# Second phase by groups of four batches: q and k of four batches per product, h1 parts in a ring, mean of x1 from a sum, plain projections at the end

## The chip, the cores and the metric

The kernel runs on one core of one Trainium2 chip. The metric is the device time of one execution in microseconds (us), as the median of several runs. Lower is better.

## The reference, cut to what matters

The input `x` has 128 batches of 128 rows and 512 columns. Two layers follow each other. The first normalises each row, mixes the rows of a batch with the 128x128 matrix `adj`, and multiplies by a 512x512 weight. The second is masked attention with 8 heads of 64 columns, a projection, and another normalisation. All is in float32.

```
h = relu(layernorm(x))
x1 = x + (adj @ h) @ w0 + b0                      # per batch
h1 = relu(layernorm(x1))
q, k, v = split(h1 @ w_qkv)                       # 8 heads of 64
s = softmax(where(adj == 0, -inf, q @ k.T / 8))   # per head, 128x128
o = concat(s @ v) @ w_proj + b_proj
out = x1 + o + layernorm(o) * gamma + beta
```

## The kernel before

**Order.** The kernel doesn't issue its instructions in the order of the source. Every piece of work is declared with `op(...)` or `dma(...)`: its engine, an estimated duration, what it reads and writes, and either a place in TensorE's time (`at`) or a due time (`due`). `Plan.schedule` then plays the pieces against those estimates and picks, on each engine, the ready piece with the earliest due time; `Plan.emit` issues them in that order. On the chip the order of each engine is fixed. Only semaphores for data and for reused buffers make an engine wait; `after=` and the estimates only shape the order.

**Buffers.** `G` lists pools of tile names. A `buf("qk", ...)` takes a name of its pool when the planner comes to it and gives it back after its last use. `t0` to `t29` are 2 KB per partition, `f0` to `f9` 4 KB, `b0` to `b7` are the eight banks of PSUM.

**Precision.** A large product is made from three products of shortened float32 values (`float32r`, called `HALF` here). The left side is split into parts h, l and s (`split_left`: one ScalarE copy, two VectorE instructions), the weights likewise (`split_weights`). `times_weights` (L398) runs 3 x 4 matmuls of 512 columns into two PSUM tiles, and `sum_up` (L414) joins these with two VectorE instructions.

**Phase 1** (`phase1`) takes the batches one after the other: load, statistics, relu, mix (L439), product with `w0` (L405), sum (L416, L418), and a store of x1 to a scratch tensor in device memory (`x1d`). In the first four batches the product is made in plain float32 instead: four matmuls per batch, which the profile shows as eight records (L448).

**Phase 2** (`phase2_pair`, L474) takes two batches at a time. x1 is loaded again (`xn in`). Statistics come from two passes of ScalarE over each batch: a sum (L374) and a sum of squares about the mean (L376), each followed by a read of the accumulator. h1 is transposed by a trip through device memory (`exchange`, L459: one DMA out, four in) and a 32x32 block transpose on VectorE (L503), and is split into hh, hl and hs of a pair (L505, L509, L506). Then come:

- q and k (L522): 4 products, each 2 halves x 3 parts x 4 = 24 matmuls of 256 columns (two batches side by side), 96 per pair; sums L529 and L530;
- v (L405 with `wv`): 12 matmuls of 512 columns per batch; sums L536, L537;
- scores (L550, small tiles), the mask added (L559), the maximum (L564), the exponentials (L571: eight per batch), the division (L576);
- the trip of the softmax through device memory (`e out`, `e in`) and a transpose (L585); in the last pair four TensorE transposes per half instead (L593);
- attend (L603, small tiles), two pairs later, then the split L392, L393, L394, the projection (L405 with `wA`), the sums L416, L418, and the tail of the batch: `x1 in`, statistics (L360 to L370), L619 to L625, store. In the last two pairs gamma and the last addition are on VectorE (L627, L629).

`T1` and `T2` are the planner's periods for a batch of phase 1 (3.7) and a pair of phase 2 (26.6). All DMAs are issued from SP.

Of the kernel before, what the change touches and what calls it, by code (L numbers as in the profile page):

```python
# [52 lines left out]
class Op:  # L53
    __slots__ = ("eng", "us", "fn", "at", "due", "prio", "bufs", "preds", "succ", "n", "ready", "start", "end", "id", "lands", "what", "tiled")


class Plan:

# [8 lines left out]
    def op(self, eng, us, fn, r=(), w=(), at=None, due=None, lands=None, what="", after=(), tiled=False):  # L67
        o = Op()
        o.eng, o.us, o.fn, o.at, o.due, o.lands, o.what, o.tiled = eng, us, fn, at, due, lands, what, tiled
        o.id, o.preds, o.succ, o.bufs = len(self.ops), set(after), [], []  # L70
# [29 lines left out]
    def schedule(self):  # L100
        p = self.p
        for o in self.ops:
            o.n, o.ready = len(o.preds), 0.0
            for x in o.preds:
                x.succ.append(o)
# [10 lines left out]
        free = dict.fromkeys(self.ENGINES, 0.0)  # L116
        for o in self.ops:
            if not o.n:
                heapq.heappush(pending[o.eng], (0.0, o.id))
        events, t, pipe, order, tiled = [0.0], 0.0, 0.0, [], False  # L120
# [68 lines left out]
    "rate": 200e3, "landing": 2.2, "lag": 0.15, "slack": 0.4, "slot": 0.15, "turn": 0.15, "stay": 2.0,  # L189
# [5 lines left out]
def kernel(  # L195
# [35 lines left out]
    def named(prefix, *numbers):  # L231
# [4 lines left out]
        "x": group(named("t", 0, 8) + named("t", 24, 27) + ["t29"]), "h0": group(named("t", 27, 29)), "y": group(named("t", 10, 16)),  # L236
        "raw": group(named("t", 16, 20)), "raw0": group(named("t", 20, 24)),
        "qk": group(named("t", 0, 8)), "xn": group(named("t", 8, 10)), "op": group(named("t", 10, 16)),
        "hx": group(named("t", 16, 18)), "ht": group(named("t", 18, 20)),
        "v": group(named("t", 20, 25) + ["t29"]), "o": group(named("t", 25, 27)), "x1b": group(named("t", 27, 29)),  # L240
        "hp": group(named("f", 0, 5)), "s": group(named("f", 5, 7)), "sx": group(named("f", 7, 8)),
        "pT": group(named("f", 8, 10)),
        "st": group(named("m", 0, 8)), "st2": group(named("l", 0, 4)), "mx": group(named("n", 0, 8)),
# [103 lines left out]
    broadcast(b0_b, b0, -4)  # L347


    def stats(srcs, how, place, due=None, plain=False):  # L350

        w = len(srcs)
        t = buf(place, [P, 24])
# [335 lines left out]
```

## Time and profile before

| | |
|---|---|
| median of 3 runs | 2218.36 us (2216.33 to 2219.66) |
| the profiled execution | 2219.66 us, span of its instructions 2217.9 us |
| granted TensorE clock in it | 0.997 |
| busy | PE 99%, PEld 88%, DVE 84%, ACT 68%, POOL 63% |
| DMA | 53.3% of 16 engines, 170 GB/s |

The times inside the profile belong to one execution. PE is TensorE's matmuls, PEld its weight loads, DVE VectorE, ACT ScalarE, POOL GpSimd, SP the engine that issues the DMAs. Matmuls overlap in their pipeline and the ends of their records are modelled. So the time of a stretch is read from the starts: the start of the next row less the start of this one. A row `x96` of the timeline is a merged run of 96 instructions.

### The profile page before, as it was taken

Reading aid. Unit: us, or ns where it says so; the run is one execution under the profiler, and the core shown is the slowest. Engines: PE = TensorE matmul, PEld = TensorE weight load, DVE = VectorE, ACT = ScalarE, POOL = GpSimd, SP = SyncE. Lnnn points to the kernel's source line nnn. Section 1 sums busy time; section 2 is a strip of 40 time slices with the busy share of each in tenths; the row PEclk is TensorE's granted clock in tenths of the full one; section 3 lists DMA queues with packets and bytes.
Section 4 is the critical chain, followed back from the end, with each engine's and each line's share of the span. In section 5 each row is a group of like instructions: output and inputs, shape, how many; then the busy total and the mean of one; then the engine's idle time right before and its main releaser. Section 6 shows DMA issues by size and latency. Waiting matters only on the chain.

```text
span 2217.9 us, 46318 instructions
## 1 busy us (share of the span) xinstructions
PE 2195.8 (99%) x15907; PEld 1946.6 (88%) x15907; DVE 1858.7 (84%) x3127; ACT 1518.1 (68%) x4368; POOL 1401.6 (63%) x1154
## 2 busy tenths in 40 slices
PE   9999999999999999999999999999999999999997
PEld 7888888888888999888899999999888899998995
DVE  6877777776888888888888888888888988888888
ACT  7887777766666666666666666666666666666662
POOL 4444444433677766767776666677777777666666
PEclk9999999999999999999999999999999999999999
DMA  5544444534555656555555555555555555555553
GB/s 193 172 153 148 144 144 143 172 133 134 172 171 172 189 175 192 180 178 181 177 175 182 185 181 174 180 177 174 179 174 183 182 176 172 180 172 174 184 166 95
DMA packets 278875, 376.43 MB, mean 170 GB/s; under 512 B 30960, under 2 KB 161136, under 8 KB 278640
## 3 DMA queue, kind: packets, MB, share of 16 engines
q1 hardware_dynamic: 278640, 373.48, 53.3%
q8 instruction: 125, 2.05, 0.4%
q14 instruction: 110, 0.90, 0.1%
HBM read 206.64 MB, written 166.72 MB: 168 GB/s over the span
## 4 chain that ended last, share of the span: by engine, by line
PE 97%; DVE 1%; DMA 1%; POOL 1%; issue 0%; SPq 0%; POOLq 0%; ACT 0%; DVEq 0%; ACTq 0%
PE b L405 47%; PE b L522 34%; PE b L550 6%; PE b L603 5%; PE b L439 5%; DMA t<-in_x_dram 1%; PE b L448 1%; POOL t L621 0%; DVE f L559 0%; DMA t<-x1d 0%; POOL t L625 0%; SPq L261 0%; DVE l L370 0%; DVE l L360 0%; POOL t L619 0%
## 5 line engine op out<-in xcount | busy, mean ns | idle before, releaser
L522 PEld LDWEIGHTS b<-f,wqk 128*128 128x128 f32 x6144 | 753.8, 192 | 18.6 <-ACT t L392 9.8
L522 PE MATMUL b<-f,wqk 128*128 128x256 f32 x6144 | 768.3, 284 | 0.0
L405 PE MATMUL b<-wA,t 128*128 128x512 f32 x3024 | 761.3, 398 | 6.6 <-DVE t L394 2.8
L405 PEld LDWEIGHTS b<-wA,t 128*128 128x128 f32 x3024 | 547.4, 188 | 121.1 <-DVE t L393 4.0
L571 ACT ACTIVATE f<-f,n 128x128 f32<-128x128 f32 x1024 | 396.8, 391 | 2.2
L405 PE MATMUL b<-wv,f 128*128 128x512 f32 x1536 | 363.9, 392 | 2.6 <-DVE f L506 1.6
L405 PEld LDWEIGHTS b<-wv,f 128*128 128x128 f32 x1536 | 287.9, 188 | 67.2 <-ACT f L505 1.9
L576 POOL TENSOR_TENSOR f<-f,n 128x1024 f32<-128x1024 f32 x128 | 245.5, 1918 | 144.0 <-DVE n L575 138.0
L392 ACT ACTIVATE t<-b 128x512 fp32r<-128x512 f32 x252 | 149.6, 594 | 207.4 <-PE b L603 104.4
L433 POOL TENSOR_TENSOR t<-t,b_b 128x512 f32<-128x512 f32 x128 | 166.7, 1303 | 181.2 <-ACT t L431 181.0
L529 ACT ACTIVATE t<-b 128x512 f32<-128x512 f32 x256 | 152.2, 594 | 183.9 <-PE b L522 183.8
L621 POOL TENSOR_TENSOR t<-t,t 128x512 f32<-128x512 f32 x128 | 174.4, 1362 | 160.4 <-DVE t L418 156.6
L619 POOL TENSOR_TENSOR t<-t,beta_b 128x512 f32<-128x512 f32 x128 | 167.9, 1312 | 137.1 <-DMA t<-x1d 137.1
L393 DVE TENSOR_TENSOR t<-b,t 128x512 fp32r<-128x512 f32 x252 | 171.6, 681 | 77.1 <-ACT t L392 77.1
L530 DVE TENSOR_TENSOR t<-b,t 128x512 f32<-128x512 f32 x256 | 172.8, 679 | 75.3 <-PE b L522 72.2
L418 DVE TENSOR_TENSOR t<-b,t 128x512 f32<-128x512 f32 x252 | 173.9, 690 | 49.4 <-PE b L405 48.8
L571 ACT ACTIVATION_READ_ACCUMULATOR f<-f,n 128x1 f32 x1024 | 194.6, 190 | 0.0
L509 POOL TENSOR_TENSOR f<-t,f 128x512 fp32r<-128x512 f32 x128 | 178.7, 1415 | 20.8 <-ACT f L505 16.6
L376 ACT ACTIVATE junk<-t,m 128x512 bf16<-128x512 f32 x250 | 180.1, 720 | 6.2
L624 POOL TENSOR_TENSOR t<-t,gamma_b 128x512 f32<-128x512 f32 x124 | 161.1, 1299 | 32.7 <-ACT t L623 32.6
L394 DVE SCALAR_TENSOR_TENSOR t<-t,b 128x512 fp32r<-128x512 f32 x252 | 170.7, 677 | 0.0
L625 POOL TENSOR_TENSOR t<-t,t 128x512 f32<-128x512 f32 x124 | 160.4, 1293 | 9.6
(84 smaller groups left out, 3029.5 us busy)
## 6 DMA issues: line engine op xcount, KB each, us to landing
t<-x1d SPq DMA_DIRECT2D x256, 256.0 KB, 4.1
d<-f SPq DMA_DIRECT2D x126, 512.0 KB, 3.2
f<-d SPq DMA_DIRECT2D x504, 128.0 KB, 3.1
t<-in_x_dram SPq DMA_DIRECT2D x128, 256.0 KB, 2.8
x1d<-t SPq DMA_DIRECT2D x128, 256.0 KB, 2.0
d<-t SPq DMA_DIRECT2D x128, 256.0 KB, 3.2
t<-d SPq DMA_DIRECT2D x512, 64.0 KB, 3.3
out_dram<-t SPq DMA_DIRECT2D x128, 256.0 KB, 2.2
```

The costliest lines, as they stand in the source:

```text
L376: op("ACT", 0.91, lambda n=n, src=src: nc.scalar.activation(junk.ap, src.ap, AF.Square, bias=t.ap[:, n:n + 1], accum_out=t.ap[:, 4 + n:5 + ...
L393: op("DVE", 0.69, lambda: nc.vector.tensor_tensor(l.ap, p.ap, h.ap.bitcast(F32), op=ALU.subtract), r=[p, h], w=[l], what=name + "l")
L394: op("DVE", 0.69, lambda: nc.vector.scalar_tensor_tensor(s.ap, h.ap.bitcast(F32), UP, p.ap, op0=ALU.mult, op1=ALU.subtract), r=[p, h], w=[ ...
L405: nc.tensor.matmul(p.ap, lhsT=t[0].ap[:, c] if t[1] is None else t[0].ap[:, c, t[1], :], rhs=w.ap[:, m, c, :], start=start and c == 0, sto ...
L418: op("DVE", 0.69, lambda: nc.vector.tensor_tensor(dst.ap, b.ap, dst.ap, op=ALU.add), r=[b], w=[dst], due=at + 4.5, what=what)
L509: op("POOL", 1.35, lambda n=n, ht=ht: nc.gpsimd.tensor_tensor(hl.ap[:, :, n, :], ht.ap, hh.ap[:, :, n, :].bitcast(F32), op=ALU.subtract), ...
L522: nc.tensor.matmul(p.ap[:, half, :], lhsT=wqk.ap[:, which, c, col:col + P], rhs=src.ap[:, c].rearrange("p b n -> p (b n)"), start=start an ...
L530: op("DVE", 0.69, lambda r=r, b=b: nc.vector.tensor_tensor(r.ap, b.ap, r.ap, op=ALU.add), r=[b], w=[r], due=tg + 5, what="qkB")
L571: nc.scalar.activation(v[:, h], v[:, h], AF.Exp, bias=mx.ap[:, h:h + 1], scale=scale, accum_out=mx.ap[:, H + h:H + h + 1])
L576: op("POOL", 1.93, lambda heads=heads, mx=mx: nc.gpsimd.tensor_tensor(heads().rearrange("p h q r -> p q h r"), heads().rearrange("p h q r ...
L619: op("POOL", 1.32, lambda x1=x1: nc.gpsimd.tensor_tensor(x1.ap, x1.ap, beta_b.ap, op=ALU.add), r=[beta_b], w=[x1], due=tl, what="beta")
L621: op("POOL", 1.32, lambda x1=x1, o=O[n]: nc.gpsimd.tensor_tensor(x1.ap, x1.ap, o.ap, op=ALU.add), r=[O[n]], w=[x1], due=tl + (3 if left > ...
```

## The change

Phase 2 takes four batches at a time (`phase2_group`), `T4` = 52.3 to the planner.

- q and k: 8 products per group, each 3 parts x 4 = 12 matmuls of 512 columns over four batches, 96 per group. The moving operand is cut from one tile `hp`, a ring of three pairs. It takes two of the pairs, so it reads four runs of 128 columns.
- h1's parts live in this ring. The transpose after the exchange is in place, and hs is made from hh and hl.
- The mean of x1: phase 1's last addition also writes the sum of its row (`accum_out`); one small VectorE instruction per group scales four sums; ScalarE's sum pass of phase 2 is gone.
- The softmax (`scores_of`) and what follows it (`rest_of`) are declared apart, one group after each other. In the plan `e in` waits for a product of q and k, or for the scores. `e in` lands in the tile that is then transposed in place. `s` and `pT` share four tiles.
- The last three pairs project in plain float32 and with one sum. Gamma and the last addition are on VectorE in them, and in the last pair x1 + o too.
- Pools are cut anew, mostly smaller (`mx` 8 to 4, `st` 8 to 3, `op` 6 to 4). The planner's DMA rate goes from 200e3 to 300e3. In all the built program has 3072 q and k matmuls for 6144, 4488 for 4560 of L405's kind, and 24 plain ones.

```diff
-    "rate": 200e3, "landing": 2.2, ...
+    "rate": 300e3, "landing": 2.2, ...
...
-        "qk": group(named("t", 0, 8)), "xn": group(named("t", 8, 10)), "op": group(named("t", 10, 16)),
-        "hx": group(named("t", 16, 18)), "ht": group(named("t", 18, 20)),
...
-        "hp": group(named("f", 0, 5)), "s": group(named("f", 5, 7)), "sx": group(named("f", 7, 8)),
-        "pT": group(named("f", 8, 10)),
+        "qk": group(named("t", 0, 8)), "v": group(named("t", 8, 14)), "op": group(named("t", 14, 18)),
+        "o": group(named("t", 18, 20)), "xn": group(named("t", 20, 22)), "hx": group(named("t", 22, 24)), "x1b": group(named("t", 24, 26)),
+        "s": group(named("f", 0, 4), fifo=False), "pT": group(named("f", 0, 4), fifo=False), "raw1": group(named("f", 2, 4)),
...
+    hp = const.tile([P, 3, 2, 3, C, P], HALF, name="hp")
-    T1, T2 = 3.7, 26.6
+    T1, T4 = 3.7, 52.3
...
+            op("DVE", 0.75, lambda: nc.vector.scalar_tensor_tensor(dst.ap, b.ap, 1.0, dst.ap, op0=ALU.mult, op1=ALU.add, accum_out=mean(i)),
+               r=[b], w=[dst, (means, i)], due=at + 4.5, what=what)
...
+    HP = {(i, m): Buf(group([f"hp{i % 6}{m}"]), lambda _, i=i, m=m: hp[:, i // 2 % 3, i % 2, m]) for i in range(B) for m in range(3)}
...
+            exchange(flat[n], C * R, 256, "h1")(flat[n])
+            op("DVE", 0.71, lambda h1=h1: nc.vector.transpose(h1.ap, h1.ap), w=[h1], what="h1T")
...
+            op("DVE", 0.7, lambda h=h, l=l, s=s: nc.vector.scalar_tensor_tensor(s(), h().bitcast(F32), 1.0 / K, l().bitcast(F32), op0=ALU.mult, op1=ALU.subtract),
...
-        for g, (kind, m) in enumerate((k, m) for m in range(2) for k in range(2)):
-            r = QK[kind, m] = buf("qk", [P, 2, 2 * P])
-            def run(p, src, which, start, stop, kind=kind, m=m):
-                for half in range(2):
-                    col = kind * D + (2 * m + half) * P
-                    for c in range(C):
-                        nc.tensor.matmul(p.ap[:, half, :], lhsT=wqk.ap[:, which, c, col:col + P],
-                                         rhs=src.ap[:, c].rearrange("p b n -> p (b n)"),
...
+        for g in range(8):
+            kind, m = g % 2, g // 2
+            r = QK[kind, m] = buf("qk", [P, D])
+            def run(p, which, start, stop, col=kind * D + m * P):
+                for c in range(C):
+                    nc.tensor.matmul(p.ap, lhsT=wqk.ap[:, which, c, col:col + P], rhs=hp[:, pick, :, which, c, :],
+                                     start=start and c == 0, stop=stop and c == C - 1)
...
+            if g == 4:
+                gate = [b.writers[-1][1]]
...
+            if rank > 2:
+                parts = split_left(PO[n], "op")
+                a, b = times_weights([(q, None, lambda q=q: q.ap) for q in parts], wA1, at_proj[n], "proj")
+                sum_up(o, a, b, bp_b, at_proj[n], "o")
+            else:
+                y, a = buf("op", [P, C, P]), buf("ps", [P, D])
+                op("ACT", 0.6, lambda y=y, p=PO[n]: nc.scalar.copy(y.ap, p.ap), r=[PO[n]], w=[y], what="oph")
+                def plain(a=a, y=y):
+                    for c in range(C):
+                        nc.tensor.matmul(a.ap, lhsT=y.ap[:, c], rhs=raw2[c].ap, start=c == 0, stop=c == C - 1)
+                op("PE", 3.43, plain, r=[y] + raw2, w=[a], at=at_proj[n], what="proj")
+                op("DVE", 0.69, lambda o=o, a=a: nc.vector.tensor_tensor(o.ap, a.ap, bp_b.ap, op=ALU.add), r=[a, bp_b], w=[o], due=at_proj[n] + 4, what="o")
```

## The prediction

> **What bounds the kernel now.** I read busy times first, then the windows by stage, then TensorE's timeline, which gives the durations.
>
> ```profile
> PE 2195.8 (99%) x15907; PEld 1946.6 (88%) x15907; DVE 1858.7 (84%) x3127; ACT 1518.1 (68%) x4368; POOL 1401.6 (63%) x1154
> ```
>
> TensorE is busy all the time. A modelled matmul end makes that number weak alone, so the windows (start, end, length, then busy time of each engine) must show where it holds:
>
> ```profile
> 488.00:553.00 65.00, 63.18 (x503) 57.66 (x503) 45.16 (x70) 45.93 (x139) 17.49 (x13) 1.00 0.46 143
> 554.00:2177.00 1623.00, 1622.19 (x12673) 1462.68 (x12671) 1412.06 (x2310) 1092.80 (x3384) 1136.73 (x915) 1.00 0.57 177
> 2177.00:2217.90 40.90, 25.52 (x156) 17.88 (x152) 36.27 (x62) 12.13 (x43) 27.94 (x23) 0.92 0.27 87
> ```
>
> In the 1623 us of the steady second phase TensorE misses 0.8 us; VectorE is next with 87%. The first phase is the same (465.4 of 466.0). Only the entry of phase 2 (1.8 us) and the last 41 us have TensorE waiting; there VectorE is busy 36.3 of 40.9. One period of a pair, from scores to scores:
>
> ```profile
> 1001.75 2.06 PE L550 MATMUL b<-t,t 64*128 64x128 f32 x32
> 1003.74 1.97 PE L603 MATMUL b<-f,t 128*64 128x128 f32 x32
> 1005.63 2.18 PE L522 MATMUL b<-f,wqk 128*128 128x256 f32 x16
> 1007.65 1.09 PE L405 MATMUL b<-wA,t 128*128 128x512 f32 x4
> 1008.58 3.99 PE L522 MATMUL b<-f,wqk 128*128 128x256 f32 x32
> 1012.41 2.02 PE L405 MATMUL b<-wA,t 128*128 128x512 f32 x8
> 1014.27 5.92 PE L522 MATMUL b<-f,wqk 128*128 128x256 f32 x48
> 1020.02 2.94 PE L405 MATMUL b<-wA,t 128*128 128x512 f32 x12
> 1022.79 5.65 PE L405 MATMUL b<-wv,f 128*128 128x512 f32 x24
> 1028.37 2.06 PE L550 MATMUL b<-t,t 64*128 64x128 f32 x32
> ```
>
> By starts, a pair takes 26.62 us: scores 1.99, attend 1.89, q and k 2.02 + 3.83 + 5.75 = 11.60, projections and v (48 matmuls) 11.13. So 512 columns cost 0.232 us and 256 columns 0.120 us (3.83 / 32). The first 16 after attend take 2.02 for 1.92: a change from small to full tiles costs about 0.1.
>
> The plain product of phase 1 and the end, with idle time and its releaser in brackets:
>
> ```profile
> 27.90 3.65 PE L448 MATMUL b<-t,t 128*128 128x512 f32 x8
> 31.38 1.05 PE L439 MATMUL b<-adjT,t 128*128 128x128 f32 x8
> ...
> 2177.10 1.19 PE L405 MATMUL b<-wA,t 128*128 128x512 f32 x4
> 2179.50 5.44 PE L405 MATMUL b<-wA,t 128*128 128x512 f32 x20 [1.21 <-DVE t L393]
> 2208.79 1.20 PE L405 MATMUL b<-wA,t 128*128 128x512 f32 x4 [2.13 <-DVE t L394]
> ```
>
> A plain product is 3.48 us by starts. The end: from 2177.10 to TensorE's last end, 2209.99, are 32.9 us. The work in them is 72 matmuls of 512 columns (16.7), two attends (3.8) and 16 transposes (2.4), 22.9 together. So 10.0 us are waits, for the split of the left side on VectorE above all; 7.9 us follow TensorE's last end.
>
> **What the Trainium skill says.** (1) "TensorE: Matmul & The Clock Gate", section "Back-to-back issue gap", gives the isolated gap as N / 2.4 + 2.5 ns: 109 ns for 256 columns, 216 for 512. Two of 256 for one of 512 would then save the fixed 2.5 ns alone. The trace differs: 120 and 232, so 8 ns are saved. The trace's numbers are used. (2) "SBUF — State Buffer", section "Who interferes with whom": a VectorE instruction with two SBUF inputs and a GpSimd instruction that reads SBUF lock each other out for a whole instruction. The trace agrees: L506 has two SBUF inputs and takes 679 ns in the median, but up to 2344:
>
> ```profile
> L506 DVE SCALAR_TENSOR_TENSOR f<-f,t x128: 645/679/2344, 486.4 to 2144.7; 128x512 fp32r<-128x512 f32 x128
> ```
>
> The same table gives TensorE its own ports for the moving operand and the weights. (3) "VectorE: DVE Perf Modes", section "Two Vector instructions with no wait between them": an op that writes out its accumulator is two instructions. No VectorE row before does this; ScalarE's read of an accumulator takes 189 ns.
>
> **The change part by part.**
>
> *q and k.* Before, 96 x 0.120 = 11.52 per pair, 23.04 per four batches. After, 96 x 0.232 = 22.27. That saves 0.77 per group, 24.7 over 32 groups. In the built program's order, attend of the second pair stands apart from its scores (scores, 4 of v, 8 of q and k, 4 of v, attend), so a group has three returns from small tiles for two: +0.1, 3 us in 31 groups. Net **-22**. The new period should be 192 x 0.232 + 7.76 + 0.24 = 52.5 us for 53.24. The moving operand now comes in four runs of 128 columns; no row before reads so. I take nothing for it (own port, one column after the other); from 0 to 4 ns per matmul, as one run's start can hardly cost more than the 8 ns won, it is 0 to +12.
>
> *Mean from a sum.* ScalarE loses 128 x (0.623 + 0.189) = 104 us, TensorE nothing, as ScalarE has 530 us to spare in 1623. VectorE gains a read in each of 128 batches of phase 1: priced as ScalarE's 0.19, 24 us, so 75% there becomes 80%, beneath a TensorE that is 99.9% busy; at 0.06 or 0.3 it is still hidden. Per group one small VectorE instruction (0.15). Cost 0; without the cover it is 0.19 per batch.
>
> *Ring, in-place transposes, hs from hh and hl.* The same instructions of about the same length: VectorE 1412 us / 61 pairs = 23.1 per pair, 46.5 per group of 52.5, 88%. ScalarE falls to 63%, GpSimd stays at 71%. hs now waits for hl (GpSimd, 1.4) also. The second pair of a group can't be split until v of the pair in its place is done: that is 12 v, 24 others and scores before its first use, over 10 us for some 5 us of splitting. Cost 0, up to 0.4 per group.
>
> *e in moved.* SP issues 52 DMAs per group, at 0.43 us 22 of 52.5. The first pair's e in stands behind the second pair's first e out, which waits for a GpSimd division; behind it wait a store and the next h1 out. From that division to both transposed tiles: 8 issues (3.4), landing (3.1), two transposes (2.5), 9 us. By the built order attend follows q and k's start by 31.6 us (128 matmuls and an attend), the division by about 15. Slack some 7 us: cost 0. If the queue is held by that much, each us late is a us per group. The 1 MB for the second copy of w_proj lands in a stretch with DMA 57% busy: 0.
>
> *Entry of phase 2.* Nothing to attend yet, so group 1's q and k follow after 37.4 us (96 + 48 matmuls, scores). Before, 1.8 us of waits for h1's parts; after 0 to 6, I take 2: 0.
>
> *The end.* Six batches plain: 6 x (3.48 - 12 x 0.232) = +4.2. VectorE loses l, s and one sum in each, 6 x 2.05 = 12.3, and gains gamma, out (two batches) and x1 + o: 4.4. The waits of 10.0 become about 3 (0 to 8), since a plain product needs only a ScalarE copy. After TensorE's last end: one sum less, about -1 of 7.9. Together **-4** (-8 to +2).
>
> Sum: -22 + 0 - 4 = **-26**. The span becomes 2192; the profiled execution (2219.66, 1.76 beyond its span) lies 1.3 above the median of the runs shown, so the median goes from 2218.4 to **2192**.
>
> **The rivals.**
>
> *A, forecast:* TensorE stays the bound; 2192, own range 2181 to 2200.
>
> *B, part of it lost:* small waits come back in each group, since the pools are smaller and the stretch of v, projection and scores (about 21 us) bunches VectorE's work. At 0.4 us per group, 13 us: 2205. For it: VectorE at 88%. Against: at 87%, TensorE missed 0.8 us in 1623.
>
> *C, slower:* VectorE falls out of step around the scores. Two scores take four PSUM banks and attend two of eight; v and projections take two per product. Banks come free only by VectorE's mask and sum instructions, in their order. One port collision there (L506 shows up to 1.7 us) holds every matmul behind the next bank. It decides at 0.8 us per group, where the gain is gone; at 1.3 per group, 42 us less the 26, it is 2234. For it: an order from estimates that know no lock, now with hs behind hl. Against: the order before came from the same estimates and held.
>
> *D, the wide product isn't cheaper:* the four runs cost the 8 ns. Then only the end gains, +3 for the third return: 2217. Against: nothing in the profile shows such a cost.
>
> **How the numbers follow.** A 0.60, B 0.18, C 0.17, D 0.05 (most of it just faster, 0.03 of it same). A change within 0.2% (4.4 us) can hardly be told from none in this kernel. Faster 0.79, same 0.04, slower 0.17. The range is 2180 to 2217: below, the q and k gain without a third return and an end at -8; above, B and D. C lies outside.
>
> **What would show it.** Right: the page's q and k group with 3072 records; 96 in 22.3 us by starts; scores of a first pair every 52.5 us; no releaser on PE above some us in phase 2; projections of the last six batches at 3.48 with short waits. Wrong: a q and k matmul of 0.236 or more (D); a PE wait on VectorE or ScalarE repeating in each group at the same place (B to 0.8 us, C above); a window of phase 2 with VectorE over 95%; waits for e in before L669.

## The result, and the profile after

The changed kernel takes 2233.77 us in the median of 4 runs (2229.43 to 2239.14), against 2218.23 for the kernel before: 1.0072 of it, interval 1.0048 to 1.0095. It is **slower** by 0.7%, and the prediction (2192, range to 2217) was wrong. The profiled execution took 2229.43 us (span 2227.4), 4.3 below the median, the fastest of the four. Inside the profile the loss is therefore 9.8 us, not 15.5.

Busy times, from the page of the kernel after:

```profile
PE 2194.1 (99%) x12811; PEld 1779.6 (80%) x12811; DVE 1871.6 (84%) x3273; ACT 1416.7 (64%) x4110; POOL 1382.1 (62%) x1148
```

The shares are close to those of before, apart from ScalarE (68% before) and the weight loads (88%). The windows (start, end, length, then busy time of PE, PEld, DVE, ACT, POOL, clock, DMA share, GB/s) for phase 1, the entry of phase 2, 28 whole groups, and the end:

```profile
22.00:487.40 465.40, 465.40 (x2496) 393.75 (x2497) 357.28 (x811) 353.51 (x769) 211.81 (x191) 1.00 0.47 155
487.40:605.34 117.94, 117.94 (x669) 95.53 (x667) 91.36 (x145) 76.45 (x228) 55.27 (x43) 1.00 0.51 155
605.34:2111.54 1506.20, 1491.44 (x8962) 1203.04 (x8961) 1316.65 (x2128) 923.61 (x2913) 1034.19 (x840) 1.00 0.59 177
2111.54:2227.40 115.86, 102.48 (x606) 74.83 (x604) 90.62 (x147) 48.40 (x173) 70.49 (x58) 0.97 0.46 136
```

TensorE misses nothing in phase 1 and at the entry, but 14.8 us in the 28 groups, where it missed 0.8 in the whole steady phase before. (The ends of matmuls are modelled, so this idle time is the smaller figure; read from the starts, the waits below come to 23 us.) A group takes 1506.20 / 28 = 53.79 us, for 53.24 before and 52.5 predicted. TensorE's timeline over most of one group, idle time and releaser in brackets:

```profile
1158.67 2.06 PE L628 MATMUL b<-t,t 64*128 64x128 f32 x32
1160.65 1.19 PE L437 MATMUL b<-wv,hp 128*128 128x512 f32 x4
1161.68 2.03 PE L571 MATMUL b<-hp,wqk 128*128 128x512 f32 x8
1163.55 1.09 PE L437 MATMUL b<-wv,hp 128*128 128x512 f32 x4
1165.74 1.97 PE L687 MATMUL b<-f,t 128*64 128x128 f32 x32 [1.10 <-DVE t L607]
1167.64 4.00 PE L571 MATMUL b<-hp,wqk 128*128 128x512 f32 x16
1171.47 1.10 PE L437 MATMUL b<-wA,t 128*128 128x512 f32 x4
1172.41 2.02 PE L571 MATMUL b<-hp,wqk 128*128 128x512 f32 x8
1174.27 2.03 PE L437 MATMUL b<-wA,t 128*128 128x512 f32 x8
1176.14 3.90 PE L571 MATMUL b<-hp,wqk 128*128 128x512 f32 x16
1179.88 2.02 PE L437 MATMUL b<-wA,t 128*128 128x512 f32 x8
1182.06 1.19 PE L437 MATMUL b<-wA,t 128*128 128x512 f32 x4 [0.16 <-DVE t L427]
1183.09 11.36 PE L571 MATMUL b<-hp,wqk 128*128 128x512 f32 x48
```

Two places wait, and they are the same ones from group to group, though not in every group. The first is attend of the second pair: its bank still holds a sum of v that VectorE (L607) has to read. From the second scores to attend are 7.07 us here; the shortest groups have 5.90, the mean of 28 is 6.35. The second is the last of the twelve projections: its split part (L427) comes late. From the 16 of q and k ahead of them to the 48 behind them are 6.95 here, 6.89 in the mean; without a wait it is 6.51 (in e18_after_order, below).

Why VectorE is late at the first place, from its own timeline and GpSimd's:

```profile
1157.88 1.20 DVE L669 STREAM_TRANSPOSE f<-f 128x1024 f32<-128x1024 f32 x1
...
1160.52 1.78 DVE L541 SCALAR_TENSOR_TENSOR hp<-hp 128x512 fp32r<-128x512 f32 x1
1162.22 0.19 DVE L652 RECIPROCAL n<-n 128x8 f32<-128x8 f32 x1
1162.34 1.19 DVE L669 STREAM_TRANSPOSE f<-f 128x1024 f32<-128x1024 f32 x1
1163.46 0.97 DVE L386 SCALAR_TENSOR_TENSOR l<-l 128x1 f32<-128x1 f32 x1
1164.35 0.68 DVE L541 SCALAR_TENSOR_TENSOR hp<-hp 128x512 fp32r<-128x512 f32 x1
...
1165.01 0.68 DVE L607 TENSOR_TENSOR t<-b,t 128x512 f32<-128x512 f32 x1
```

```profile
1159.93 0.56 POOL L382 TENSOR_TENSOR l<-l,minus_half 128x1 f32<-128x1 f32 x1
1160.45 1.30 POOL L714 TENSOR_TENSOR t<-t,t 128x512 f32<-128x512 f32 x1
1162.49 1.92 POOL L653 TENSOR_TENSOR f<-f,n 128x1024 f32<-128x1024 f32 x1 [0.74 <-DVE n L652]
```

The view has no idle time of VectorE in this stretch. `hs` (L541) starts 0.07 us behind GpSimd's L714 (x1 + o) and takes 1.78 us, where its neighbour takes 0.68. L386, the *shift* (minus mean times rs, one over the standard deviation: **one** element per partition, two operands in SBUF), starts while L653 runs and takes 0.97, where it takes 0.15 unhindered. L607 ends at 1165.69 and attend starts at 1165.74. The times fit: L714 ends at 1161.75, and `hs` needs 0.6 from there; L653 ends at 1164.41, and L386 at 1164.43. This holds throughout: of the 127 instructions of L386 in this profile 124 start while a GpSimd instruction runs, and each of these ends 12 to 67 ns after that one. The section on order above says that only semaphores make an engine wait; here is a wait that no semaphore shows. The Trainium skill, "SBUF — State Buffer", section "Who interferes with whom", says just this: a VectorE instruction with two SBUF inputs and a GpSimd one that reads SBUF exclude each other for a whole instruction.

The second place has the same look. Between the two halves of a split stands the other shift of the group:

```profile
1179.17 0.64 DVE L426 TENSOR_TENSOR t<-b,t 128x512 fp32r<-128x512 f32 x1
1179.73 1.68 DVE L386 SCALAR_TENSOR_TENSOR l<-l 128x1 f32<-128x1 f32 x1
1181.33 0.68 DVE L427 SCALAR_TENSOR_TENSOR t<-t,b 128x512 fp32r<-128x512 f32 x1
```

```profile
1179.47 1.92 POOL L653 TENSOR_TENSOR f<-f,n 128x1024 f32<-128x1024 f32 x1 [0.15 <-issue]
```

Again it meets L653, which ran from 1179.47 to 1181.39. L386 has a mean of 952 ns after; before, its counterpart L370 has 528:

```profile
L386 DVE SCALAR_TENSOR_TENSOR l<-l 128x1 f32<-128x1 f32 x122 | 116.1, 952 | 1.8 <-POOL l L382 1.8
L370 DVE SCALAR_TENSOR_TENSOR l<-l 128x1 f32<-128x1 f32 x124 | 65.4, 528 | 0.3 <-POOL l L366 0.3
```

It holds ScalarE up as well: the wait of the last normalisation on it (L716, us in total, times, longest) is the largest in VectorE's and ScalarE's lists, where before its counterpart was 53.7 us.

```profile
ACT t L716 <- DVE l L386: 171.9, 88, 3.2
```

### The profile page after: what moved, and what is told of

Its sections match the earlier page's. It is cut to its first block, busy times and chain, and to the rows that moved or that the text cites. A ratio compares the mean times of both kernels' runs of the same rounds, so it can differ in the third digit from the quotient of the medians.

```text
span 2227.4 us, 40336 instructions
## 1 busy us (share of the span) xinstructions
PE 2194.1 (99%) x12811; PEld 1779.6 (80%) x12811; DVE 1871.6 (84%) x3273; ACT 1416.7 (64%) x4110; POOL 1382.1 (62%) x1148
## 4 chain that ended last, share of the span: by engine, by line
PE 69%; DMA 9%; DVE 9%; POOL 5%; SPq 4%; issue 2%; ACT 1%; DVEq 0%; POOLq 0%; ACTq 0%
PE b L437 31%; PE b L571 24%; PE b L478 5%; DMA t<-d 5%; PE b L687 4%; SPq L266 4%; DMA f<-d 4%; PE b L628 4%; DVE hp L541 2%; POOL t L718 1%; POOL t L717 1%; POOL hp L539 1%; DVE f L669 1%; POOL f L653 1%; DVE l L386 1%
## 5 line engine op out<-in xcount | busy, mean ns | idle before, releaser
L571 PE MATMUL b<-hp,wqk 128*128 128x512 f32 x3072 | 744.8, 396 | 0.0
L571 PEld LDWEIGHTS b<-hp,wqk 128*128 128x128 f32 x3072 | 575.1, 188 | 141.4 <-issue 5.0
L437 PEld LDWEIGHTS b<-wA,t 128*128 128x128 f32 x2952 | 543.7, 188 | 134.2 <-DVE t L427 15.5
L437 PE MATMUL b<-wv,hp 128*128 128x512 f32 x1536 | 400.5, 397 | 0.0
L437 PEld LDWEIGHTS b<-wv,hp 128*128 128x128 f32 x1536 | 283.8, 188 | 68.1 <-issue 0.2
L653 POOL TENSOR_TENSOR f<-f,n 128x1024 f32<-128x1024 f32 x128 | 245.8, 1920 | 60.8 <-DVE n L652 50.0
L714 POOL TENSOR_TENSOR t<-t,t 128x512 f32<-128x512 f32 x126 | 165.5, 1313 | 171.8 <-DVE t L448 169.4
L539 POOL TENSOR_TENSOR hp<-t,hp 128x512 fp32r<-128x512 f32 x128 | 178.9, 1399 | 107.9 <-ACT hp L538 72.0
L578 ACT ACTIVATE t<-b 128x512 f32<-128x512 f32 x256 | 150.6, 588 | 132.7 <-PE b L571 132.5
L716 ACT ACTIVATE t<-t,l 128x512 f32<-128x512 f32 x122 | 99.5, 816 | 206.6 <-DVE l L386 171.9
L579 DVE TENSOR_TENSOR t<-b,t 128x512 f32<-128x512 f32 x256 | 175.0, 684 | 50.4 <-PE b L571 46.8
L636 DVE TENSOR_TENSOR f<-b,maskb 128x512 f32<-128x512 f32 x256 | 164.1, 682 | 42.8 <-PE b L687 27.9
L472 POOL TENSOR_TENSOR t<-t,t 128x512 f32<-128x512 f32 x92 | 120.5, 1311 | 121.4 <-ACT t L470 121.3
L606 ACT ACTIVATE t<-b 128x512 f32<-128x512 f32 x128 | 75.6, 591 | 157.4 <-PE b L437 157.2
L427 DVE SCALAR_TENSOR_TENSOR t<-t,b 128x512 fp32r<-128x512 f32 x246 | 166.4, 676 | 0.0
L718 POOL TENSOR_TENSOR t<-t,t 128x512 f32<-128x512 f32 x122 | 158.0, 1295 | 2.7
```

What stands on the lines that cost most here:

```text
L427: op("DVE", 0.69, lambda: nc.vector.scalar_tensor_tensor(s.ap, h.ap.bitcast(F32), UP, p.ap, op0=ALU.mult, op1=ALU.subtract), r=[p, h], w=[ ...
L437: nc.tensor.matmul(p.ap, lhsT=parts[m][2]()[:, c], rhs=w.ap[:, m, c, :], start=start and c == 0, stop=stop and c == C - 1)
L539: op("POOL", 1.35, lambda ht=ht, h=h, l=l: nc.gpsimd.tensor_tensor(l(), ht(), h().bitcast(F32), op=ALU.subtract), r=[h1, HP[i, 0]], w=[HP[ ...
L571: nc.tensor.matmul(p.ap, lhsT=wqk.ap[:, which, c, col:col + P], rhs=hp[:, pick, :, which, c, :], start=start and c == 0, stop=stop and c = ...
L579: op("DVE", 0.69, lambda r=r, b=b: nc.vector.tensor_tensor(r.ap, b.ap, r.ap, op=ALU.add), r=[b], w=[r], due=tg + 4, what="qkB")
L636: op("DVE", 0.68, lambda e=e, heads=heads, ps=ps: nc.vector.tensor_tensor(heads()[:, e * C:(e + 1) * C], ps[e].ap.rearrange("p c (q r) -> ...
```

## The experiments

Theories, by the letters that the expectations use. **L**: VectorE's small two-operand instructions are held by GpSimd, and TensorE waits behind them. **H**: it is not the hold but the step; the chain of the statistics passes through VectorE's queue. **O**: the planner's order is at fault, which puts attend too early for VectorE. **S**: the schedule; a group leaves VectorE too little room, held or not. **D**: transfers land late and hold VectorE's queue, for which the planner's new DMA rate of 300e3 may be to blame (not the prediction's rival D). **M**: the moving operand in runs of 128 columns. "Before" was run beside each, at 2217.4 to 2218.0; brackets give the ratio to it with its 95% interval.

### Not the rate, not the runs, not the width: e3, e4, e5

*e3_rate200*, the changed kernel with the old rate:

```diff
-    "rate": 300e3, "landing": 2.2, ...
+    "rate": 200e3, "landing": 2.2, ...
```

> Only the planner's DMA rate goes back from 300e3 to 200e3, as before the change, so the order issues transfers earlier against their use. D: the waits of VectorE for DMA fall and with them those of TensorE, 2215 to 2225. L and S: within 6 us of the changed kernel, 2228 to 2240, either way.

2437.32 (1.0994, 1.098 to 1.1009). TensorE waited in total 98 us on VectorE's mask (L636) and GpSimd's hl (L539) alone. So the new rate is not at fault: the plan by groups needs it. That late transfers are not the cause either is shown by e1 and e18 below, where the waits go while VectorE still waits for transfers (L540 in e18, 28.5 us in all; L535 after, 33.2).

*e4_narrow*, the changed kernel with q and k again in 256 columns:

```diff
-                    nc.tensor.matmul(p.ap, lhsT=..., rhs=hp[:, pick, :, which, c, :], ...)
+                for half in range(2):
+                        nc.tensor.matmul(p.ap[:, half * 2 * P:(half + 1) * 2 * P], lhsT=..., rhs=hp[:, spots[half][0], :, which, c, :], ...)
```

> q and k of four batches as before the change in width: two matmuls of 256 columns for each of 512 (6144 for 3072), all else as in the changed kernel. TensorE's work grows by 192 x 0.120 - 96 x 0.2333 = 0.64 us per group, 20 us in all. If TensorE sets the pace and its waits are added to its work (L with the wait released by a chain that TensorE itself starts): 2250 to 2256. If VectorE or a DMA sets the pace of a group (S or D in the strict form), the longer products only fill waits: 2234 to 2242.

2234.87 (1.0079, 1.0065 to 1.0093), the same as after. TensorE's q and k are not even longer in it: 22.22 us per group by starts, for 22.50 after, as the run of 96 matmuls in each group takes 113.8 ns per matmul and the shorter runs 117 to 118. So the expected 20 us of extra work were not there, and this run can't say which engine sets the pace.

*e5_runs_before*, the kernel before with its parts laid out as `[2][C][128]`, so that its q and k too read runs of 128:

```diff
-        hh, hl, hs = (buf("hp", [P, C, 2, P], HALF) for _ in range(3))
+        hh, hl, hs = (buf("hp", [P, 2, C, P], HALF) for _ in range(3))
```

> The kernel before, with h1's parts laid out as [2 batches][4 chunks][128] for [4][2][128]: q and k's matmuls of 256 columns read two runs of 128 columns for one run of 256; products, widths and engines' work are the same. In the run with narrow products such a matmul took 113.4 to 117.8 ns by starts where the kernel before takes 120. If the layout of the moving operand sets that (theory M): 96 matmuls x 2 to 6.5 ns is 0.2 to 0.6 us per pair, 13 to 40 us, 2180 to 2205, less what VectorE's 87% then hold up. If it is the place of the weights or of PSUM or the run of instructions (theory N): 120 ns as before, 2214 to 2222.

2217.51 (0.9999, 0.9991 to 1.0007), 119.8 ns per matmul as before. M falls.

### The small instructions: e1, e2

*e1_shift_pool*: both shifts (L386 and the pair's L415) to GpSimd; VectorE makes the negative mean in a one-input instruction.

```diff
-            op("DVE", 0.16, lambda: nc.vector.scalar_tensor_tensor(shift(), mv()[:, :, 0], -1.0, rs(), ...),
+            op("POOL", 0.55, lambda: nc.gpsimd.tensor_tensor(shift(), neg(), rs(), op=ALU.mult),
...
-        op("DVE", 0.16, lambda: nc.vector.tensor_tensor(shift(), means.ap[:, first:first + w], rs(), op=ALU.mult),
+        op("POOL", 0.7, lambda: nc.gpsimd.tensor_tensor(shift(), means.ap[:, first:first + w], rs(), op=ALU.mult),
```

> The small product shift = -mean * rs of the two statistics (VectorE, two SBUF inputs, mean 952 and 589 ns in the changed kernel where its own work is about 150) goes to GpSimd, behind the power there; VectorE gets a one-input negation of about 145 ns instead. Theory L (VectorE's instructions with two SBUF inputs are held by GpSimd's, so VectorE frees PSUM late and attend waits, 0.76 us per group): VectorE gets some 4 us per group back, the waits of attend fall below 0.3, 28 groups x 0.5 is 14 us, 2218 to 2224. Theory D (h1's and the softmax's way back through SP lands late and holds VectorE's queue, 1.4 us per group of waits for DMA): no change, 2230 to 2238. Theory S (the group's order has too little room for VectorE in itself, locks or not): 2228 to 2236.

2208.53 (0.9958, 0.9945 to 0.9971): 25 us less than after, more than the 10 to 16 that L forecast, and faster than before. S had 2228 to 2236 and D 2230 to 2238. The wait on the sum of v at attend falls from 11.1 us to 3.0.

*e2_durations*: the planner is told what the three VectorE instructions took on average.

```diff
-            op("DVE", 0.16, lambda: nc.vector.scalar_tensor_tensor(shift(), mv()[:, :, 0], ...
+            op("DVE", 0.95, lambda: nc.vector.scalar_tensor_tensor(shift(), mv()[:, :, 0], ...
...
-        op("DVE", 0.16, lambda: nc.vector.tensor_tensor(shift(), means.ap[:, first:first + w], ...
+        op("DVE", 0.59, lambda: nc.vector.tensor_tensor(shift(), means.ap[:, first:first + w], ...
...
-            op("DVE", 0.7, lambda h=h, l=l, s=s: ...
+            op("DVE", 1.04, lambda h=h, l=l, s=s: ...
```

> Only the planner's estimates of three VectorE instructions change, to the means that the changed kernel's profile shows (shift 0.16 to 0.95 and 0.59, hs 0.70 to 1.04); the order changes with them, the work does not. L: an order that reckons with the held instructions puts attend later and lets TensorE wait less, 2215 to 2228, though the locks remain. D: no change, 2230 to 2238. S: the longer estimates leave even less room, attend moves back, no gain or slower, 2232 to 2245.

2238.27 (1.0095, 1.0082 to 1.0108). A plan with the measured means is no better: the waits move to q and k (11.7 us on ScalarE's L578), and the held L386 becomes longer still, 1143 ns. The time lies in the range given for S, not in L's 2215 to 2228. So a truer estimate doesn't repair the plan; that VectorE lacks room even without holds is refuted by e1, and again by e18.

### What the change is worth without the holds: e7, e6, e8, e12

*e7_shift_before*, the shifts put on GpSimd in the kernel **before**. The line below serves phase 1 too, so 63 shifts of phase 1 move as well, which e1 leaves on VectorE:

```diff
-            op("DVE", 0.16, lambda: nc.vector.tensor_tensor(shift(), t.ap[:, 0:w], rs(), op=ALU.mult),
+            op("POOL", 0.7, lambda: nc.gpsimd.tensor_tensor(shift(), t.ap[:, 0:w], rs(), op=ALU.mult),
```

> The kernel before with the same edit: shift of both statistics on GpSimd. L: it takes time from VectorE only (some 1.5 us per pair), and TensorE waits for nothing in the steady part of this kernel, so within 4 us of the kernel before, 2214 to 2222; the end may gain a few us, where VectorE is busy 36 of 41. If GpSimd becomes late by it: slower. If the 25 us of the same edit in the changed kernel came from anything but waits (less power drawn, fewer semaphores): 2190 to 2200.

2213.0 (0.9977, 0.9968 to 0.9986), 5 us less. They don't come from the second phase: q and k start at 481.89 us for 488.05, so 6 us are gained ahead of it, while from scores to scores a pair takes 26.65 us in the mean of 56 in both kernels. So this gain is of another kind than e1's. Against this kernel e1 is 4.5 us faster.

*e6_narrow_shift*, e1 with e4's edit (its diff is theirs together):

> The changed kernel with shift on GpSimd, and q and k in matmuls of 256 columns again. With the waits gone (PE 0.2 us per group), the width is seen on TensorE itself. By the prediction's prices (120 against 233 ns) the narrow form costs 0.64 us per group more: 2228. By the spacing of the run with narrow products (113.4 ns, the shortest distance from scores to scores 52.8 us for 53.0): 0.2 us per group less, 2200 to 2206.

2212.65 (0.9973, 0.9962 to 0.9984). e1 with the wide product is 2212.65 - 2208.53 = 4.1 us faster. In the profiles q and k take 22.87 us per group here and 22.75 in e1, 3 us in all. In e4, against after, the sign was the other way, so the width has no sure worth of its own.

*e8_split_end*, e1 without the plain projections at the end:

```diff
-            if rank > 2:
+            if True:
                 parts = split_left(PO[n], "op")
```

> The changed kernel with shift on GpSimd, and the last six batches projected in three parts with two sums again, as before the change (GpSimd and ScalarE still leave gamma and the last addition to VectorE there). The prediction had the plain form cost TensorE 4.2 us more and give back some 7 of waits and 1 at the very end: so 2211 to 2214 for 2208.5. If the plain form gives nothing: 2204 to 2208.

2213.39 (0.9979, 0.9972 to 0.9986). The plain end is worth 4.9 us; 4 were predicted.

*e12_act_mean*, e1 with ScalarE's sum pass back in place of the means from phase 1:

```diff
-        t, arg = stats(XN, "mean", "st", first=pair[0], junk=...)
+        t, arg = stats(XN, "ACT", "st", junk=...)
```

> The changed kernel with shift on GpSimd, and the mean of x1 in phase 2 from ScalarE's sum pass again (128 passes, 104 us of ScalarE; shift of phase 1's statistics on GpSimd too; the written sums are left unused). The prediction put this part at nothing: 2206 to 2212. If ScalarE's freed time matters (its copies free PSUM and open the chain of hs): slower, 2212 to 2225.

2205.33 (0.9945, 0.9932 to 0.9957), not slower than e1. (Phase 1's shifts are on GpSimd in it too.) The mean from a sum is worth nothing, as predicted.

### The price of a hold that nobody waits for: e9, e10, e11

*e9_two_input*: e1 with a VectorE instruction of the old shift's form, whose result goes nowhere. *e10_one_input*: the same with one input.

```diff
+            op("DVE", 0.16, lambda: nc.vector.scalar_tensor_tensor(t.ap[:, 14:15], t.ap[:, 12:13], -1.0, t.ap[:, 18:19], op0=ALU.mult, op1=ALU.mult), ...
```

```diff
+            op("DVE", 0.16, lambda: nc.vector.tensor_scalar(t.ap[:, 14:15], t.ap[:, 18:19], -1.0, None, op0=ALU.mult), ...
```

> The changed kernel with shift on GpSimd (2208.5), plus one instruction of one element on VectorE, after the power, that reads two SBUF operands (mean and rs) and writes a column that nobody reads: 127 times, four per group, about 150 ns of own work. TensorE's order is the same. L: it is held by GpSimd's next instruction for 0.6 to 1 us each, VectorE is late again, attend waits again: 2220 to 2232. S (only the amount of VectorE's work counts): 0.6 us per group, 2208 to 2213.

> The control of that: the same added instruction in the same place, after the same power, but with one SBUF operand (rs). L: it isn't held, mean near 150 ns, 2207 to 2213. If it is the waiting for GpSimd's power in VectorE's queue that delays, and not the lock: as slow as the run with two operands.

e9: 2207.55 (0.9958, 0.9945 to 0.997), the dummy 549 ns in the mean. e10: 2204.16 (0.9939, 0.9926 to 0.9951), the dummy 134 ns. TensorE's order is the same in both. The hold alone costs 3.4 us for some 1.6 us of VectorE per group: L in its simple form (any hold costs) falls. The trace says where the dummy stands: between second scores and attend it takes 0.28 us in the mean of the groups, and its long ones come behind the sum of v that frees attend's bank (0.83) or elsewhere, as between the halves of a split, where TensorE doesn't wait in this order. e10, which only adds an instruction to e1, is 4.4 us faster than e1: the planner's order moves with every edit, so a difference of 4 us in this family can't be put down to the edit without a look at where it falls.

*e11_single*: e1, with the `ve` of a pair (variance plus epsilon) as two one-element instructions for one of two elements.

```diff
-        op("DVE", 0.17, lambda: nc.vector.tensor_scalar(ve(), t.ap[:, :w], 1.0 / D, EPS, op0=ALU.mult, op1=ALU.add),
+            for n in range(w):
+                nc.vector.tensor_scalar(t.ap[:, 16 + n:17 + n], t.ap[:, n:n + 1], 1.0 / D, EPS, op0=ALU.mult, op1=ALU.add)
```

> The changed kernel with shift on GpSimd, and the variance line of the late statistics (one VectorE instruction of two elements, mean 907 ns in that kernel, 159 in the changed one) as two instructions of one element. L, if an instruction of two elements takes the shared ports and one of one element doesn't: two times 0.15 us for 0.91, 1.2 us per group less on VectorE, the PE waits left (0.2 us per group) shrink, 2204 to 2209. If the length has another cause: both keep about 0.5 to 0.9 us, 2208 to 2216.

2204.17 (0.9939, 0.9926 to 0.9953). The instruction goes from 907 ns to 139 each. As e10 gains the same 4.4 us with the long instruction still in it (884 ns), this gain isn't shown to come from that.

### Hold, step or order: e13 to e18

*e13_hop*: both shifts stay on VectorE at their place, but in a one-input form (the other operand is a scalar per partition). *e16_hop_single* adds e11's edit.

```diff
-            op("DVE", 0.16, lambda: nc.vector.scalar_tensor_tensor(shift(), mv()[:, :, 0], -1.0, rs(), ...),
+                for n in range(w):
+                    nc.vector.tensor_scalar(t.ap[:, 20 + n:21 + n], t.ap[:, 18 + n:19 + n], t.ap[:, 12 + 2 * n:13 + 2 * n], -1.0, ...)
```

> The changed kernel with both shifts still on VectorE, in the same place and the same order on every engine, but written with one SBUF tensor (rs) and the mean as a per-partition scalar, one element at a time. L (the hold by GpSimd makes the waits): the two rows fall from 952 and 589 to about 150 ns each, the waits of attend go, 2203 to 2212. H (ScalarE's norm, first in its queue, waits for a step through VectorE's queue, hold or not): part stays, 2220 to 2230. O (the order that the planner made for the changed kernel): 2229 to 2239, as the order is the same.

> The run with both shifts in one-input form on VectorE, and the variance line of the late statistics as two one-element instructions. No small instruction is held any more, no work is moved to GpSimd. L: 2201 to 2207, at or below the best so far (2204.2). H: 2218 to 2230.

2223.26 (1.0035, 1.0022 to 1.0047) and 2223.0 (1.0028, 1.0016 to 1.0039). The shifts are quick now, 184 ns, but only 10.5 of e1's 25 us are back. That alone speaks for H or O: the step was still on VectorE, and in e1 the planner had put attend four matmuls (0.93 us) later than here.

*e14_late_only* moves only the pair's shift (L415) to GpSimd, the second change of e1's diff; *e15_norm_only* only L386, the first:

> The changed kernel with only the shift of the late statistics (relu of h1, 64 instructions, 589 ns) on GpSimd; the norm's shift (122, 952 ns) stays on VectorE. L, by time held: 0.9 of 4.1 us per group are taken away, so a quarter or less of the 24: 2226 to 2234. If the chain of h1 is what matters: 2206 to 2214.

> The other one alone: only the norm's shift on GpSimd, the late statistics' on VectorE. L, by time held: 3.2 of 4.1 us per group, most of the 24: 2208 to 2218. If the chain of h1 is what matters: 2226 to 2236. The planner's order differs most in this one (attend of the second pair stands 24 matmuls later).

2224.14 (1.003, 1.002 to 1.004) and 2211.59 (0.9975, 0.9966 to 0.9984). L386, which stands at both waiting places, is worth 22 us; but e15's order also has attend later, by four matmuls in 20 groups and by 20 in nine. e14 gains 9.6 us, a little more than expected, and 7.8 of them at the second place: the 16 to the 48 of q and k take 6.61 there for 6.89, though L386 between the halves still takes 1.68. The split is late by only 0.3 us after, and L415 had been held for up to 1.2 us ahead of it. So the second wait needs both holds, and the two gains don't add up to e1's 25. Order and instruction had to be parted:

*e17_late_attend*: the changed kernel, its instructions untouched, attend of the second pair planned 6 us later. *e18_after_order*: e1's instructions with the changed kernel's order around attend, by giving the moved pieces their old durations in the plan.

```diff
-            at_attend = [t0 + T4 + at_t[p]] * 2
+            at_attend = [t0 + T4 + at_t[p] + 6.0 * p] * 2
```

```diff
-            op("DVE", 0.17 if plain else 0.27, ve_neg, ...
+            op("DVE", 0.17, ve_neg, ...
...
-            op("POOL", 0.55, lambda: nc.gpsimd.tensor_tensor(shift(), neg(), rs(), op=ALU.mult),
+            op("POOL", 0.16, lambda: nc.gpsimd.tensor_tensor(shift(), neg(), rs(), op=ALU.mult),
...
-        op("POOL", 0.7, lambda: nc.gpsimd.tensor_tensor(shift(), means.ap[:, first:first + w], rs(), op=ALU.mult),
+        op("POOL", 0.16, lambda: nc.gpsimd.tensor_tensor(shift(), means.ap[:, first:first + w], rs(), op=ALU.mult),
```

> The changed kernel with its instructions untouched; only the planner's place for the second pair's attend is 6 us later (the given times of attend are part of the plan, not a wait). TensorE's order in a group becomes: 16 of v, second scores, 4 of v, 20 of q and k, attend, 76 of q and k with projections between, instead of 8 of q and k, 4 of v, attend. Both small two-operand instructions stay on VectorE. Theory O (the place of attend is too early for VectorE, so the waits come from the order alone): 2206 to 2216, and the wait on the sum of v before attend is gone. Theory L/H (VectorE's small instructions are held, and ScalarE's chain stands behind them, wherever attend is): 2223 or more, the waits turning up at W instead.

> The kernel of e1_shift_pool (both shifts on GpSimd) with the planner's durations of the moved instructions set back to those of the changed kernel, so that TensorE's order around the second pair's attend is that of the changed kernel: scores, 4 of v, 8 of q and k, 4 of v, attend, 16 of q and k. Theory O (order alone): the waits are back, 2218 to 2232. Theory L/H (holds and what stands behind them): 2204 to 2211, as the shifts no longer occupy VectorE.

e17: 2225.41 (1.0032, 1.0019 to 1.0045). e18: 2205.95 (0.9945, 0.9931 to 0.9958). **O falls**: the changed kernel's order alone, with the shifts on GpSimd, is fast; a later attend alone isn't, as q and k then wait (9.2 us on the sum of v, 5.3 on `hs`). In e18 the second scores follow each other at 52.96 us (28 groups, 620.80 to 2103.59). TensorE never waits at the second place, and at the first for 0.7 us in all, in the first groups. TensorE, VectorE and GpSimd in the same stretch of e18:

```profile
1150.83 2.06 PE L633 MATMUL b<-t,t 64*128 64x128 f32 x32
...
1156.73 1.97 PE L692 MATMUL b<-f,t 128*64 128x128 f32 x32
```

```profile
1149.60 1.21 DVE L674 STREAM_TRANSPOSE f<-f 128x1024 f32<-128x1024 f32 x1
...
1152.24 0.66 DVE L546 SCALAR_TENSOR_TENSOR hp<-hp 128x512 fp32r<-128x512 f32 x1
1152.82 0.19 DVE L657 RECIPROCAL n<-n 128x8 f32<-128x8 f32 x1
1152.93 1.19 DVE L674 STREAM_TRANSPOSE f<-f 128x1024 f32<-128x1024 f32 x1
1154.05 0.71 DVE L546 SCALAR_TENSOR_TENSOR hp<-hp 128x512 fp32r<-128x512 f32 x1
...
1154.81 0.68 DVE L612 TENSOR_TENSOR t<-b,t 128x512 f32<-128x512 f32 x1
1155.40 1.16 DVE L416 TENSOR_SCALAR m<-m 128x2 f32<-128x2 f32 x1
```

```profile
1151.67 0.54 POOL L387 TENSOR_TENSOR l<-l,minus_half 128x1 f32<-128x1 f32 x1
1152.29 0.66 POOL L391 TENSOR_TENSOR l<-l 128x1 f32<-128x1 f32 x1
1152.91 1.30 POOL L719 TENSOR_TENSOR t<-t,t 128x512 f32<-128x512 f32 x1
...
1157.12 0.19 POOL L391 TENSOR_TENSOR l<-l 128x1 f32<-128x1 f32 x1
```

From the start of the first softmax transpose to the end of the sum that frees attend's bank VectorE needs 1155.49 - 1149.60 = 5.89 us; after needed 1165.69 - 1157.88 = 7.81. The shift on GpSimd (L391) sits between the power (L387) and x1 + o (L719), so `hs` comes first and is done in 0.66. VectorE is held here too (L416, 1.16 us), but only behind the sum.

VectorE's timeline in the same stretch of e13, and GpSimd's division:

```profile
1155.67 1.20 DVE L675 STREAM_TRANSPOSE f<-f 128x1024 f32<-128x1024 f32 x1
...
1158.31 1.77 DVE L547 SCALAR_TENSOR_TENSOR hp<-hp 128x512 fp32r<-128x512 f32 x1
...
1161.23 0.17 DVE L388 TENSOR_SCALAR l<-l 128x1 f32<-128x1 f32 x1
1161.32 1.42 DVE L547 SCALAR_TENSOR_TENSOR hp<-hp 128x512 fp32r<-128x512 f32 x1
...
1162.72 0.67 DVE L613 TENSOR_TENSOR t<-b,t 128x512 f32<-128x512 f32 x1
```

```profile
1160.27 1.92 POOL L659 TENSOR_TENSOR f<-f,n 128x1024 f32<-128x1024 f32 x1 [0.74 <-DVE n L658]
```

The hold has **moved**: with L388 out of the way in 0.09 us, the second `hs` now meets the GpSimd division and takes 1.42. The stretch is 1163.39 - 1155.67 = 7.72 us, hardly less than after's. Over all groups of each kernel, between second scores and attend (us per group; "held" is the time of the two `hs` beyond 1.36 and of the shift beyond 0.15):

| kernel | two hs | shift | held | scores to attend, mean | q,k 16 to q,k 48 |
|---|---|---|---|---|---|
| after | 2.44 | 0.97 | 1.9 | 6.35 | 6.89 |
| e13_hop | 3.18 | 0.17 | 1.8 | 6.46 | 6.54 |
| e18_after_order | 1.41 | on GpSimd | 0.05 | 5.92 | 6.51 |

VectorE is no less busy in e18 (1309.1 of 1528.6 us, 571.4 to 2100) than in e13 (1304.3 of 1546.6, 571.4 to 2118), so it isn't the sum of its work that decides. e13's 10.5 us are the second place: (6.89 - 6.54) x 28 = 9.8. The first place stayed. H isn't needed: the step itself costs 0.09 us by starts. But e13's time lies in H's range, and a kernel with the step on VectorE and nothing held in this stretch wasn't tried. That the shifts on VectorE make the waits is shown by e1 and e18; that it is the hold and not the step is, for the first place, argued from these traces.

## Why the prediction was wrong, point by point

**The balance**, within the profiled executions and per group of the 28: predicted 52.5, measured 53.79. Of the 1.29 between them 0.46 is the floor without waits (52.96 in e18), 0.45 the wait at attend, 0.38 the wait at the projections. Against before that is (52.96 - 53.24) x 28 = -8 for the floor and +23 for the waits; all that lies outside these groups gives -6. The sum is the 9.5 between the two spans. The other runs of after were slower than its profiled one by 3 to 10 us; no profile shows which of the waits grew in them.

**q and k, -22: mis-sized, and its reason isn't shown.** q and k themselves came as forecast: 22.48 us per group in e18 for 23.21 in two pairs of before, 0.73 less, where 0.77 were reckoned. The first group's 96 matmuls, without waits:

```profile
487.40 22.57 PE L571 MATMUL b<-hp,wqk 128*128 128x512 f32 x96
509.80 2.02 PE L437 MATMUL b<-wv,hp 128*128 128x512 f32 x8
```

22.40 / 96 = 233.3 ns, for 232 assumed. What was mis-sized is the term for changes of tile kind. It was taken as 0.24 per group, 0.1 of it new, for the returns to q and k alone; but v pays too, 11.57 per group for 11.17 before, as four matmuls of v take 1.03 after scores and 1.02 before attend (e18), for 0.93 elsewhere. So the floor fell by 0.28 and not by 0.74. Nor was it shown that the width is the reason. In the new kernel's arrangement a matmul of 256 columns takes 113.4 to 117.8 ns in most runs (e4, e6), not 120, so two of them take 227 to 236 for 233.3 of the wide one: e6 against e1 gains 4.1 us by width, e4 against after nothing. Why 256 columns became cheaper stays open; the runs of 128 alone don't do it (e5). The Trainium skill ("TensorE: Matmul & The Clock Gate", section "Back-to-back issue gap") has a fixed 2.5 ns per matmul, which would be the whole worth of the width; e6's 2 x 117.8 - 233.3 = 2.3 is near that, e4's 113.4 is not, and its 216 ns for 512 columns isn't what is measured.

**"Ring, in-place transposes, hs from hh and hl: cost 0, up to 0.4 per group": the step that failed.** The working took VectorE's durations from before as a sum, 46.5 of 52.5 us, and read slack from the share. But an instruction that GpSimd holds has no fixed duration. With another order beside it the shift went from 528 to 952 ns, and it is not the share that matters (84% on both pages) but what stands behind the held instruction: the sum that frees a bank (L607) and the split of a left side (L427). The waits behind these two cost TensorE 0.83 per group, where 0 was reckoned.

**Rival C had it.** It named the place (around the scores), the resource (a PSUM bank that a VectorE sum frees), the cause (a port collision of the order of L506's) and the planner that knows no lock. It got 0.17. Its number, 2234, is met by chance: it reckoned 42 us of waits less 26; measured are 23 of waits on a smaller gain. What spoke against it, "the order before came from the same estimates and held", was weak: before too has holds (its shift takes 528 ns in the mean, 0.15 unhindered, and L506 up to 2344), only they fell where TensorE waited for nothing. The 0.83 per group lie between rival B's 0.4, which had no such cause, and C's 1.3. The prediction's rival D is right in half: by e5 and the 233.3 ns the four runs cost no 8 ns, but e4 and e6 leave open whether the wide product is cheaper at all.

**Mean from a sum, 0: right** (e12), and phase 1 is 465.40 of 465.40. (In the profile of before it is 466.00 of 466.00 from 22 to 488 us, not 465.4.) The read of VectorE's accumulator was priced at ScalarE's 0.19; it takes 83 ns (this group of the kernel after):

```profile
L450 DVE DVE_READ_ACCUMULATOR t<-b,t 128x1 f32 x88 | 7.3, 83 | 0.0
```

The section "Two Vector instructions with no wait between them" of "VectorE: DVE Perf Modes" says rightly that there are two instructions; the price is this trace's.

**e in, 0: right.** TensorE waits on the transpose of `e in` (L669) once, 2.8 us, at the end. **Entry, 0: right**, 117.94 busy of 117.94. **The end, -4: right**, -4.9 by e8; two waits of 2.8 and 2.7 us stand where 3 in all were predicted, so the pieces are less exact than the sum.

## What to carry to other kernels

Read a VectorE instruction that meets GpSimd by its own time and its held time apart (the minimum against the mean of its group), and look at what is queued behind it, not at the engine's share: a hold of 1.16 us cost TensorE nothing behind the sum that frees a bank (e18, L416), while 1.9 us of holds per group ahead of that sum cost it 0.45 in the mean. Removing one held instruction can hand the hold to the next (e13), so judge such an edit by the length of the stretch, not by the instruction. A tiny two-operand instruction on VectorE is cheap to move: with the shifts on GpSimd, and `ve` in one-element instructions (e11), this kernel runs at 2204.2 us, 0.6% below before.

## What the runs showed of the hardware

- A VectorE instruction on one element per partition with two SBUF operands takes 0.15 us when no GpSimd instruction runs at its start and had a mean of 0.95 us in the kernel after. Where one runs, it ended 12 to 67 ns after that one (124 cases).
- A `tensor_scalar` of two elements per partition, one input, is held as well (907 ns in e1), while the form of one element isn't (139 ns in e11). The section of "SBUF — State Buffer" named above says that `tensor_scalar` can enter a mode that takes both ports; that a single element keeps it out is what these two runs suggest.
- GpSimd is held in turn: its one-element shift takes 0.19 us free and 0.66 while `hs` runs (e18, L391).
- Four matmuls of 512 columns take 1.03 us right behind the small tiles of scores and 1.02 right ahead of those of attend, for 0.92 to 0.93 elsewhere (e18).
- A q and k matmul of 256 columns takes 119.8 to 126 ns in the kernel before and mostly 113.4 to 117.8 in e4 and e6; why they differ stays open.
